# Delta-rule layer on one core: 64-token products in 64x64 tiles, convolution steps issued one block later

## The chip, the core and the metric

The kernel runs on one core of a Trainium2 chip. The core has a matrix engine (TensorE; PE in the profile), a vector engine (VectorE; DVE), an activation engine (ScalarE; ACT), a general engine (GpSimd; POOL) and SyncE (SP), which here does little but issue DMA transfers. Each engine works through its own instruction queue in order; they meet through semaphores. The metric is device microseconds for one execution, first to last instruction and a little around it. Before the change the median of three runs is 2928.5 us (2926.8 to 2933.6).

## What is computed

A model of two layers on 2 x 1024 tokens of width 256, all in float32: layer 0 adds a gated delta-rule attention and a mixture-of-experts layer to the residual, layer 1 a gated linear attention and a sparsified feed-forward. The change touches only the delta rule, which for each of 32 value heads (16 key heads, each shared by two value heads) is

```python
mixed = concat([q, k, v]); y = silu(causal_conv(mixed, conv_w, KSIZE=4))   # per channel
beta = sigmoid(b); g = -exp(A_log) * softplus(a + dt_bias)
q = l2norm(q) * DK ** -0.5; k = l2norm(k)                                  # repeated for 2 value heads
def step(S, inp):
    qt, kt, vt, gt, bt = inp
    S = S * exp(gt)[:, None, None]
    kv = einsum('hk,hkv->hv', kt, S)
    delta = (vt - kv) * bt[:, None]
    S = S + kt[:, :, None] * delta[:, None, :]
    return S, einsum('hk,hkv->hv', qt, S)
gated = core * silu(z); gated *= rsqrt(mean(gated ** 2) + EPS); out = (gated * norm_w) @ W_out
```

The kernel doesn't step through tokens. It takes 64 tokens at a time and solves what they do to one another with the inverse of a unit lower triangular 64x64 matrix.

## The kernel before

Layer 0's expert part runs from about 70 to 257 us of the span, the delta rule from 257 to about 2610, layer 1 after that.

The delta rule goes over 8 groups of heads (4 value heads, 2 key heads, written m). In a group the 1024 tokens of both batches are cut into 4 units of 256 tokens, a unit into 2 pairs, a pair into 2 chunks. A chunk holds 64 tokens of each batch: batch 0 on partitions 0 to 63 (`LO`), batch 1 on 64 to 127 (`HI`). That makes 64 pairs, 128 chunks. Every pair passes through these steps, in generators that give way after a few instructions:

- `conv_block`: four projections pj per pair (L152), copied by ScalarE into `raw` (L356) behind three old columns (GpSimd, L347), scaled by the last tap (ScalarE, L358), then three multiply-adds on VectorE (L363), then silu (L372, issued by the next block's `silu_pending`).
- `gates_part`: in odd pairs the sums of squares of q and k (`unit_sums`: products ssr, a copy, four transposes ss) and from them the norms on GpSimd (`unit_norms`, rn at L447); then two z projections.
- `pair_scores`: decay lb (scan L508, L510, L512), products kq, the matrices np (L526; index 0 keys by keys, index 1 queries by keys, which the output product uses), and DMAs on SyncE that lay np out anew: nat (L530), natd through DRAM (L536) and n8 (L540).
- `pair_lanes`: the inverse of all 8x8 diagonal blocks on VectorE (X at L558 to E at L582), spread by two DMAs (ed, U; L584, L586).
- `pair_inverse`: the ladder from 8 to 64: px, xs, pyt, U, and a transpose L of U at each rung (L603 to L645), the last rung with px (L660), xs (L663), pyt (L669) and copies into `invT`.
- `chunk_tokens`: keys by tokens, scaled (ktok, L688), values by tokens (vtok, L697).
- `chunk_state`: pks and pqs from state S (L716), four updates of vtok (L719), S times decay (GpSimd, L724), pf = invT x vtok (L734), f (ScalarE), pS (L743), po (L747), S plus pS (L754), qs, z (L758, L760).
- `chunk_output`, `chunk_project`: mean of squares (L765, ms at L775), root, scaling z (L782), transposes yT, projection out (L798), residual (L800).

pf multiplies with a 128x128 matrix whose two 64x64 blocks are the batches' inverses and whose other blocks are zero. po uses 64x64 blocks as they are, both batches at once.

`in_windows` (L823) sets the program's order. Each generator has a window in the pair's time (0 to 1), its steps are spread evenly over it, and the generator whose next step is due first issues it. The tile framework's scheduler then places each instruction on its engine; `tc.issue_after(x)` keeps what is issued inside it behind x on the engine. `k.anchor` is the latest convolution step; the scan (L508) and the first X (L558) are kept behind it. PSUM is one pool of 8 banks of 128x512, handed out in turn to every product (`ps_tile`).

Of the kernel before, what the change touches and what calls it, by code (L numbers as in the profile page):

```python
# [9 lines left out]
F32 = mybir.dt.float32  # L10
# [139 lines left out]
def project(k, ps, lhsT_of, rhs_of):  # L150
    for kt in range(KT):
        k.nc.tensor.matmul(ps, lhsT_of(kt), rhs_of(kt), start=(kt == 0), stop=(kt == KT - 1))  # L152
# [27 lines left out]
def delta_gates(k, pool, I):  # L180
# [66 lines left out]
    for b, rows in enumerate((LO, HI)):  # L247
        ps = ps_tile(k, f"sum_end{b}")
        nc.tensor.matmul(ps, k.ones[rows], flat(g)[rows], start=True, stop=True)
        nc.scalar.activation(flat(k.eEnd[:, b]), ps, AF.Exp)  # L250
        yield
# [75 lines left out]
def conv_block(k, pools, h, m, i):  # L327
# [31 lines left out]
    if h.part < NPART - 1:  # L359
        nc.gpsimd.tensor_copy(k.tails[:, at], raw[:, :, HALF // NB :])  # L360
    for j in range(KSIZE - 1):
        shifted = raw[:, :, j : j + HALF // NB]
        k.anchor = nc.vector.scalar_tensor_tensor(y, shifted, tap(j), y, ALU.mult, ALU.add).ins  # L363
        yield
    k.pending.append((out.rearrange("p (c b i) -> p b c i", b=NB, i=CT), chunks(y)))
# [10 lines left out]
def conv_part(k, pools, p, n):  # L376
# [9 lines left out]
    for v, m, i in blocks[n : n + 2]:  # L386
        if 0 <= v < NUNIT:
            yield from conv_block(k, pools, k.units[v], m, i)


def gates_part(k, pools, p):

    u, odd = divmod(p, 2)
    if odd and u + 1 < NUNIT:
# [3 lines left out]
        yield from unit_sums(k, pools, k.units[u + 1])  # L398
        unit_norms(k, pools, k.units[u + 1])
        yield  # L400
    if 0 <= p - 1 < NPAIR:
        for x in k.pairs[p - 1].chunks:
            chunk_gate(k, pools, x)
            yield


def chunk_gate(k, pools, x):
# [4 lines left out]
    project(k, ps, lambda kt: k.xnT[:, kt, t0 : t0 + P], lambda kt: w[:, kt].rearrange("p m c -> p (m c)"))  # L412
    x.z = pools.z.tile([P, HPG, P], F32, tag="z", name=f"z{x.name}")
    nc.scalar.activation(x.z.rearrange("p h d -> p (h d)"), ps, AF.Silu)

# [12 lines left out]
def unit_sums(k, pools, h):  # L428
# [7 lines left out]
    yield  # L436
    ps = ps_tile(k, f"ss{h.name}").rearrange("p (c a) -> p c a", c=UCHUNK)
    for c in range(UCHUNK):
        nc.tensor.transpose(ps[:, c, :], of_chunk(rows, c), k.ident)
# [49 lines left out]
def pair_scores(k, pools, pr):  # L489
# [8 lines left out]

    nc, wk, h = k.nc, pools.work, pr.h
# [110 lines left out]
def pair_inverse(k, pools, pr):  # L610
# [20 lines left out]
    nc.vector.transpose(flat(L), flat(U))  # L631
    yield
    for s in (3, 4):
# [11 lines left out]
        nc.vector.transpose(flat(L), flat(U))  # L645
# [7 lines left out]
    for n, r in enumerate(QUARTERS):  # L653
        (nc.gpsimd.tensor_copy, nc.scalar.copy)[n % 2](invT[r, :, r], U[r])
# [15 lines left out]
    for q, copy in ((0, nc.scalar.copy), (2, nc.vector.tensor_copy)):  # L670
        copy(invT[QUARTERS[q], :, QUARTERS[q + 1]], pyt[QUARTERS[q]])
# [3 lines left out]
def chunk_tokens(k, pools, x):  # L675

    nc, wk, h, c = k.nc, pools.work, x.h, x.c
    if not x.last:
# [22 lines left out]
def chunk_state(k, pools, x):  # L701

    nc, wk, h, c = k.nc, pools.work, x.h, x.c
# [5 lines left out]
    if not x.first:  # L709
        pks, pqs = four(k, f"pks{x.name}"), four(k, f"pqs{x.name}")  # L710
        for s, out in ((0, pks), (1, pqs)):
            for m in range(KPG):
                two = slice(2 * m, 2 * m + 2)
                for b, rows in halves:
                    q = of_chunk(h.kq[m][:, s], c, b)
                    nc.tensor.matmul(out[rows, two, :], q, k.S[:, b, two, :], start=True, stop=True)  # L716
        yield
        for i in range(HPG):
            nc.vector.scalar_tensor_tensor(  # L719
                x.v[:, i, :], pks[:, i, :], at(k.neG, i), x.v[:, i, :], ALU.mult, ALU.add  # L720
            )
# [10 lines left out]
    pf = four(k, f"pf{x.name}")  # L732
    for i in range(HPG):
        nc.tensor.matmul(pf[:, i, :], invT[:, i, :], x.v[:, i, :], start=True, stop=True)  # L734
    f = wk.tile([P, HPG, P], F32, tag="f", name=f"f{x.name}")
    nc.scalar.copy(f, pf)  # L736
    yield
    if not x.last:
        pS = [four(k, f"pS{x.name}_{b}") for b in range(NB)]
        for i in range(HPG):  # L740
            for b, rows in halves:
                for cols in (LO, HI):
                    nc.tensor.matmul(pS[b][cols, i, :], x.k[rows, i, cols], f[rows, i, :], start=True, stop=True)  # L743
# [721 lines left out]
```

## Time and profile before

| | us |
|---|---|
| median of three runs | 2928.5 (2926.8 to 2933.6) |
| profiled execution | 2937.13 |
| its span, first to last instruction | 2935.4 |
| mean granted TensorE clock | 0.969 |
| pj, 1024 matmuls | 529.5 busy |
| convolution steps L363, 768 | 692.6 busy, 188.0 idle ahead |
| pf, 1024 records | 153.0 busy, 29.8 idle ahead |
| po, 2048 records | 135.1 busy |
| pS, 3840 records | 132.5 busy, 12.6 idle ahead |
| px (L603), 8192 records | 102.1 busy, 143.1 idle ahead |
| ktok on GpSimd, 120 | 142.7 busy |
| np on VectorE, 128 | 82.0 busy |

"Busy" is the time in which the engine worked on that group. "Idle ahead" is the time that the engine stood still just before instructions of the group. TensorE splits an fp32 product into passes, which the profile lists as records of their own: one 128x128 by 128x128 product gives two. The records of one engine overlap a little (pipelining), so what a group takes of the path is read from its start to the start of the next group on the same engine. In a timeline a row reads: start us, duration us, engine, line, operation, output<-inputs, shape, count, and in brackets the idle time before it and who ended it.

### The profile page before, as it was taken

How to read it: one execution, taken by the hardware profiler on the slowest of the kernel's cores; microseconds unless marked ns; L12 is line 12 of the kernel's file. 1: busy time of each engine (PE TensorE's matmuls, PEld its weight loads, DVE VectorE, ACT ScalarE, POOL GpSimd, SP SyncE). 2: the span in 40 equal slices, each digit the busy share in tenths (PEclk: the TensorE clock that was granted, in tenths of full speed). 3: DMA queues.
4: the chain of work that ended last, by engine and by line, in shares of the span. 5: the costliest groups of instructions: out<-in, count | busy, mean ns of one | idle time of the engine just before them, and what ended most of it. 6: DMA issues, size and time to landing. Idle time of an engine off the chain costs nothing.

```text
span 2935.4 us, 87796 instructions
## 1 busy us (share of the span) xinstructions
PE 2642.3 (90%) x36502; PEld 1673.8 (57%) x36502; DVE 1938.2 (66%) x3845; ACT 1713.7 (58%) x4121; POOL 1542.9 (53%) x2690
## 2 busy tenths in 40 slices
PE   5998689999999899989998999999999989989997
PEld 2444356665666566656665666566555655654565
DVE  7652566766777677767776776677677767645544
ACT  4432566666666666666676666666666666544321
POOL 2222466666666666666666666566666666630000
PEclk9998899999999999999999999999999999999999
DMA  3001111111111111111111111111111111110000
GB/s 77 4 1 58 37 27 32 39 36 35 36 36 44 26 35 37 44 28 43 30 41 28 42 36 35 28 42 36 41 23 37 31 34 25 24 60 0 1 15 15
DMA packets 265966, 95.22 MB, mean 32 GB/s; under 512 B 220513, under 2 KB 244193, under 8 KB 265569
## 3 DMA queue, kind: packets, MB, share of 16 engines
q1 hardware_dynamic: 261872, 86.67, 13.2%
q8 instruction: 287, 4.70, 0.7%
q10 hardware_dynamic: 3696, 2.95, 0.4%
q14 instruction: 111, 0.90, 0.1%
HBM read 53.63 MB, written 27.53 MB: 28 GB/s over the span
## 4 chain that ended last, share of the span: by engine, by line
PE 49%; DVE 18%; POOL 13%; ACT 6%; issue 6%; DMA 4%; SPq 4%; DVEq 0%; POOLq 0%; ACTq 0%
PE pj L152 9%; DVE conv L363 5%; PE out L798 4%; PE z L152 4%; POOL rn L447 3%; PE pks L716 3%; POOL S L724 2%; PE pS L743 2%; SPq L540 2%; PE px L603 2%; PE pf L734 2%; DMA natd<-np 2%; PE y L1083 2%; PE pg L152 2%; DVE qs L758 2%
## 5 line engine op out<-in xcount | busy, mean ns | idle before, releaser
L363 DVE SCALAR_TENSOR_TENSOR conv<-raw,convw,conv 128x512 f32<-128x512 f32 x768 | 692.6, 903 | 188.0 <-ACT conv L358 127.7
L152 PE MATMUL pj<-xnT,w 128*128 128x512 f32 x1024 | 529.5, 643 | 8.7 <-DMA w<-in_W_qkvz 8.7
L152 PEld LDWEIGHTS pj<-xnT,w 128*128 128x128 f32 x1024 | 192.6, 201 | 193.2 <-issue 185.8
L719 DVE SCALAR_TENSOR_TENSOR vtok<-pks,neG,vtok 128x128 f32<-128x128 f32 x480 | 142.3, 343 | 218.4 <-PE pks L716 217.6
L724 POOL TENSOR_TENSOR S<-S,eEnd 128x512 f32<-128x512 f32 x224 | 261.5, 1184 | 31.9 <-PE pqs L716 20.8
L765 ACT ACTIVATE gsq<-z 128x128 f32<-128x128 f32 x512 | 156.8, 306 | 194.2 <-DVE z L760 186.2
L798 PE MATMUL out<-wo,yTs 128*128 128x256 f32 x1024 | 253.6, 391 | 1.4 <-ACT yTs L788 1.4
L152 PE MATMUL z<-wz,xnT 128*128 128x512 f32 x512 | 246.8, 605 | 0.0
L356 ACT COPY raw<-pj 128x512 f32<-128x512 f32 x256 | 148.0, 578 | 152.3 <-PE pj L152 139.3
L603 PE MATMUL px<-L,natm 32*32 32x32 f32 x8192 | 102.1, 200 | 143.1 <-DVE L L645 124.7
L347 POOL COPY raw<-tails 128x6 f32<-128x6 f32 x192 | 75.2, 392 | 249.1 <-DVE conv L363 242.6
L798 PEld LDWEIGHTS out<-wo,yTs 128*128 128x128 f32 x1024 | 187.6, 193 | 26.2 <-ACT yTs L788 1.9
L603 PEld LDWEIGHTS px<-L,natm 32*32 32x32 f32 x8192 | 88.5, 111 | 168.5 <-issue 83.1
L734 PE MATMUL pf<-vtok,invT 128*128 128x128 f32 x1024 | 153.0, 287 | 29.8 <-DVE vtok L719 27.3
L358 ACT ACTIVATE conv<-pj,convw 128x512 f32<-128x512 f32 x256 | 177.0, 692 | 0.0
L754 DVE TENSOR_TENSOR S<-S,pS 128x512 f32<-128x512 f32 x224 | 145.8, 682 | 33.4 <-POOL S L724 25.5
L729 ACT ACTIVATE qs<-pqs,neG 128x128 f32<-128x128 f32 x480 | 136.5, 367 | 48.9 <-PE pqs L716 48.9
L734 PEld LDWEIGHTS pf<-vtok,invT 128*128 128x128 f32 x1024 | 129.9, 192 | 45.7 <-DVE vtok L719 30.8
L447 POOL TENSOR_TENSOR rms<-ms,mhalf 128x4 f32<-128x4 f32 x128 | 148.7, 1162 | 9.9
L782 POOL TENSOR_TENSOR z<-z,rms 128x512 f32<-128x512 f32 x128 | 142.8, 1116 | 10.0
L743 PE MATMUL pS<-f,ktok 64*64 64x128 f32 x3840 | 132.5, 275 | 12.6 <-ACT f L736 12.6
L688 POOL TENSOR_TENSOR ktok<-kt,wend 128x512 f32<-128x512 f32 x120 | 142.7, 1189 | 0.8 <-ACT kt L684 0.8
(323 smaller groups left out, 5775.9 us busy)
## 6 DMA issues: line engine op xcount, KB each, us to landing
lb<-grows SPq DMA_DIRECT2D x128, 128.0 KB
natd<-np SPq DMA_DIRECT2D x128, 128.0 KB
w<-in_W_qkvz SPq DMA_DIRECT2D x16, 512.0 KB
nat<-np SPq DMA_DIRECT2D x256, 32.0 KB
n<-natd SPq DMA_DIRECT2D x512, 4.0 KB
ed<-E SPq DMA_DIRECT2D x64, 128.0 KB
U<-ed SPq DMA_DIRECT2D x64, 128.0 KB
wz<-in_W_qkvz SPq DMA_DIRECT2D x16, 256.0 KB
```

Source lines behind the costliest of these rows:

```text
L152: k.nc.tensor.matmul(ps, lhsT_of(kt), rhs_of(kt), start=(kt == 0), stop=(kt == KT - 1))
L356: nc.scalar.copy(chunks(raw[:, :, KSIZE - 1 :]), pv)
L358: nc.scalar.activation(chunks(y), pv, AF.Copy, scale=tap(KSIZE - 1))
L363: k.anchor = nc.vector.scalar_tensor_tensor(y, shifted, tap(j), y, ALU.mult, ALU.add).ins
L447: nc.gpsimd.tensor_tensor(out, x, k.mhalf[:, 0 : x.shape[1]], ALU.pow)
L603: k.nc.tensor.matmul(out[r, i, :], lhsT[r, i, :], rhs[r, i, :], start=True, stop=True)
L724: nc.gpsimd.tensor_tensor(k.S[:, b], k.S[:, b], bcast(k.eEnd[:, b, t, h.h0 : h.h0 + HPG], 2, P), ALU.mult)
L734: nc.tensor.matmul(pf[:, i, :], invT[:, i, :], x.v[:, i, :], start=True, stop=True)
L743: nc.tensor.matmul(pS[b][cols, i, :], x.k[rows, i, cols], f[rows, i, :], start=True, stop=True)
L754: nc.vector.tensor_tensor(k.S[:, b], k.S[:, b], pS[b], ALU.add)
L765: nc.scalar.activation(sq, x.z[:, i, :], AF.Square, accum_out=x.sumsq[:, i : i + 1])
L798: nc.tensor.matmul(po[:, 0:D], x.yT[:, i, :], wo[:, i, :], start=(i == 0), stop=(i == HPG - 1))
```

## The change

1. pf and po become eight products each in 64x64 tiles, at all four places of the array: rows by the half r that the inputs lie in, columns by the half r^m that the output goes to. Both are written to one PSUM tile `fo` of two banks (bank m holds key head m) from a pool of its own; the other pool shrinks from 8 to 6 banks, and each stage has its own. invT keeps only its 64x64 blocks.
2. As key head 1's results land in the other half, its state is kept with the halves crossed: `eEnd` is written in four operations, pks and pqs read `S[:, b ^ m]`. Half of ktok and half of the second np are computed into helper tiles (ktoko, npo), by two operations of half the size, and two DMAs of SyncE each carry them to the other half: 120 chunks and 64 pairs.
3. The convolution steps of a block are issued after the next block's evacuation (`convolve`), and behind `k.chain`: the ladder's last L or the last vtok update. conv1 is cut into conv1 and conv2.
4. In odd pairs a z projection is issued between ssr and the transposes ss, which stay behind it on TensorE.

Instructions in the program, before and after: TensorE matmuls 19075, 19587; VectorE tensor_tensor 1656, 1720; GpSimd tensor_tensor 1753, 1873; SyncE DMA issues 1235, 1603; ScalarE activations two more.

The diff at its core; hunks of the same kind and small ones are left out:

```diff
@@ -247,7 +248,10 @@
     for b, rows in enumerate((LO, HI)):
         ps = ps_tile(k, f"sum_end{b}")
         nc.tensor.matmul(ps, k.ones[rows], flat(g)[rows], start=True, stop=True)
-        nc.scalar.activation(flat(k.eEnd[:, b]), ps, AF.Exp)
+        by_key = lambda a: a.rearrange("p (t g m j) -> p t g m j", t=NTILE, g=NGROUP, m=KPG)
+        for m in range(KPG):
+            mine = by_key(flat(k.eEnd[:, b ^ m]))[:, :, :, m]
+            nc.scalar.activation(mine, by_key(ps)[:, :, :, m], AF.Exp)
         yield
     for name in ("neG", "nrev"):
         nc.vector.tensor_scalar(sums[name], sums[name], -1.0, None, ALU.mult)
@@ -358,11 +362,24 @@
     nc.scalar.activation(chunks(y), pv, AF.Copy, scale=tap(KSIZE - 1))
     if h.part < NPART - 1:
         nc.gpsimd.tensor_copy(k.tails[:, at], raw[:, :, HALF // NB :])
+    yield from convolve(k)
+    k.projected = y, raw, tap, (out.rearrange("p (c b i) -> p b c i", b=NB, i=CT), chunks(y))
+def convolve(k):
+    if not k.projected:
+        return
+    y, raw, tap, silu = k.projected
     for j in range(KSIZE - 1):
         shifted = raw[:, :, j : j + HALF // NB]
-        k.anchor = nc.vector.scalar_tensor_tensor(y, shifted, tap(j), y, ALU.mult, ALU.add).ins
+        with ExitStack() as behind:
+            if k.chain:
+                behind.enter_context(k.tc.issue_after(k.chain))
+            k.anchor = k.nc.vector.scalar_tensor_tensor(y, shifted, tap(j), y, ALU.mult, ALU.add).ins
         yield
-    k.pending.append((out.rearrange("p (c b i) -> p b c i", b=NB, i=CT), chunks(y)))
+    k.projected = None
+    k.pending.append(silu)
 def silu_pending(k):
@@ -383,25 +400,34 @@
         blocks = [(u + 1, 1, 0), (u + 1, 1, 1), (u + 1, 0, 2), (u + 1, 0, 3)]
     else:
         blocks = [(u + 1, 0, 0), (u + 1, 0, 1), (u, 1, 2), (u, 1, 3)]
-    for v, m, i in blocks[n : n + 2]:
+    for v, m, i in blocks[n : n + count]:
         if 0 <= v < NUNIT:
             yield from conv_block(k, pools, k.units[v], m, i)
+        elif k.projected:
+            yield from convolve(k)
+            silu_pending(k)
 def gates_part(k, pools, p):
     u, odd = divmod(p, 2)
+    chunks = k.pairs[p - 1].chunks if 0 <= p - 1 < NPAIR else []
+    gate = None
     if odd and u + 1 < NUNIT:
         for m in range(KPG):
             unit_squares(k, pools, k.units[u + 1], m)
             yield
-        yield from unit_sums(k, pools, k.units[u + 1])
+        rows = unit_sums(k, pools, k.units[u + 1])
+        yield
+        for x in chunks[0:1]:
+            gate = chunk_gate(k, pools, x)
+            yield
+        unit_turned(k, k.units[u + 1], rows, gate)
         unit_norms(k, pools, k.units[u + 1])
         yield
-    if 0 <= p - 1 < NPAIR:
-        for x in k.pairs[p - 1].chunks:
-            chunk_gate(k, pools, x)
-            yield
+    for x in chunks[1:] if gate else chunks:
+        chunk_gate(k, pools, x)
+        yield
 def chunk_gate(k, pools, x):
@@ -433,10 +460,18 @@
         nc.tensor.matmul(ps[r, :], k.ones[:, r], sq, start=True, stop=True)
     rows = pools.sq.tile([P, HALF], F32, tag="sq", name=f"ssr{h.name}")
     nc.scalar.copy(rows, ps)
-    yield
+    return rows
+def unit_turned(k, h, rows, ahead):
     ps = ps_tile(k, f"ss{h.name}").rearrange("p (c a) -> p c a", c=UCHUNK)
-    for c in range(UCHUNK):
-        nc.tensor.transpose(ps[:, c, :], of_chunk(rows, c), k.ident)
+    with ExitStack() as behind:
+        if ahead:
+            behind.enter_context(k.tc.issue_after(ahead))
+        for c in range(UCHUNK):
+            k.nc.tensor.transpose(ps[:, c, :], of_chunk(rows, c), k.ident)
     h.ss = ps.rearrange("p c (m i r) -> p c m i r", m=KPG, i=2)[:, :, :, :, 0]
@@ -521,11 +557,15 @@
     yield
     pr.np = pools.np.tile([P, 2, PC, HPG, CT], F32, tag="np", name=f"np{pr.name}")
     pairs = lambda a: a.rearrange("p x (m j) i -> p (x m) j i", m=KPG)
-    for s in range(2):
-        by = kq[:, :, :, s].rearrange("p x m i -> p (x m) i")
-        nc.vector.tensor_tensor(pairs(pr.np[:, s]), pairs(lb), bcast(by, 2, 2), ALU.mult)
-        if s == 0:
-            yield
+    by = kq[:, :, :, 0].rearrange("p x m i -> p (x m) i")
+    nc.vector.tensor_tensor(pairs(pr.np[:, 0]), pairs(lb), bcast(by, 2, 2), ALU.mult)
+    yield
+    other = wk.tile([P, PC, 2, CT], F32, tag="npo", name=f"npo{pr.name}", bufs=1)
+    for m, out in enumerate((pr.np[:, 1, :, 0:2], other)):
+        two = slice(2 * m, 2 * m + 2)
+        nc.vector.tensor_tensor(out, lb[:, :, two], bcast(kq[:, :, m, 1], 2, 2), ALU.mult)
+    for rows, across in ((LO, HI), (HI, LO)):
+        nc.sync.dma_start(pr.np[across, 1, :, 2:4], other[rows])
     for n, r in enumerate(QUARTERS):
         nc.sync.dma_start(pr.nat[r], pr.np[r, 0, :, :, QUARTERS[n % 2]])
@@ -628,7 +668,7 @@
     U = pr.U
     join = masked(3)
     L = new("L", 3)
-    nc.vector.transpose(flat(L), flat(U))
+    k.chain = nc.vector.transpose(flat(L), flat(U)).ins
     yield
     for s in (3, 4):
         px = part(k, f"px{s}_{pr.name}", B)
@@ -651,7 +691,7 @@
     invT = pr.invT.rearrange("p x h c -> p (x h) c")
     full = pr.np[:, 0].rearrange("p x h c -> p (x h) c")
     for n, r in enumerate(QUARTERS):
-        (nc.gpsimd.tensor_copy, nc.scalar.copy)[n % 2](invT[r, :, r], U[r])
+        (nc.gpsimd.tensor_copy, nc.scalar.copy)[n % 2](invT[r, :, QUARTERS[n % 2]], U[r])
     yield
     px = part(k, f"px5_{pr.name}", B)
     for i in range(PH):
@@ -683,9 +724,12 @@
         kt = wk.tile([P, KPG, P], F32, tag="kt", name=f"kt{x.name}", bufs=1)
         nc.scalar.copy(kt, pk[:, 0:KPG, :])
         x.k = wk.tile([P, HPG, P], F32, tag="ktok", name=f"ktok{x.name}")
-        pair = lambda a: a.rearrange("p (m i) c -> p m i c", m=KPG)
-        wend = h.wend[:, c, :].rearrange("p (m i) -> p m i", m=KPG)
-        nc.gpsimd.tensor_tensor(pair(x.k), bcast(kt, 2, 2), bcast(wend, 3, P), ALU.mult)
+        other = wk.tile([P, 2, P], F32, tag="ktoko", name=f"ktoko{x.name}")
+        for m, out in ((1, other), (0, x.k[:, 0:2])):
+            wend = h.wend[:, c, 2 * m : 2 * m + 2]
+            nc.gpsimd.tensor_tensor(out, bcast(kt[:, m], 1, 2), bcast(wend, 2, P), ALU.mult)
+        for rows, across in ((LO, HI), (HI, LO)):
+            nc.sync.dma_start(x.k[across, 2:4], other[rows])
         yield
     pv = four(k, f"pv{x.name}")
     for i in range(HPG):
@@ -713,12 +761,12 @@
                 two = slice(2 * m, 2 * m + 2)
                 for b, rows in halves:
                     q = of_chunk(h.kq[m][:, s], c, b)
-                    nc.tensor.matmul(out[rows, two, :], q, k.S[:, b, two, :], start=True, stop=True)
+                    nc.tensor.matmul(out[rows, two, :], q, k.S[:, b ^ m, two, :], start=True, stop=True)
         yield
         for i in range(HPG):
-            nc.vector.scalar_tensor_tensor(
+            k.chain = nc.vector.scalar_tensor_tensor(
                 x.v[:, i, :], pks[:, i, :], at(k.neG, i), x.v[:, i, :], ALU.mult, ALU.add
-            )
+            ).ins
         if not x.last:
             for b in range(NB):
                 nc.gpsimd.tensor_tensor(
@@ -729,22 +777,33 @@
             nc.scalar.activation(qs[:, i, :], pqs[:, i, :], AF.Copy, scale=at(k.neG, i))
         yield
-    pf = four(k, f"pf{x.name}")
-    for i in range(HPG):
-        nc.tensor.matmul(pf[:, i, :], invT[:, i, :], x.v[:, i, :], start=True, stop=True)
+    fo = k.psum2.tile([P, KPG, 2, 2, P], F32, tag="fo", name=f"fo{x.name}")
+    pf, po = fo[:, :, 0], fo[:, :, 1]
+    across = lambda r, m: halves[r ^ m][1]
+    for i in range(2):
+        for m in range(KPG):
+            for r, rows in halves:
+                n = 2 * m + i
+                nc.tensor.matmul(pf[across(r, m), m, i, :], invT[rows, n, :], x.v[rows, n, :], start=True, stop=True)
     f = wk.tile([P, HPG, P], F32, tag="f", name=f"f{x.name}")
-    nc.scalar.copy(f, pf)
+    by_key = lambda a: a.rearrange("p (m i) d -> p m (i d)", m=KPG)
+    flat = lambda a: a.rearrange("p m i d -> p m (i d)")
+    nc.scalar.copy(by_key(f), flat(pf))
     yield
     if not x.last:
-        pS = [four(k, f"pS{x.name}_{b}") for b in range(NB)]
+        pS = [four(k, f"pS{x.name}_{r}") for r in range(NB)]
         for i in range(HPG):
-            for b, rows in halves:
+            for r, rows in halves:
                 for cols in (LO, HI):
-                    nc.tensor.matmul(pS[b][cols, i, :], x.k[rows, i, cols], f[rows, i, :], start=True, stop=True)
-    po = four(k, f"po{x.name}")
-    for i in range(HPG):
-        for b, rows in halves:
-            nc.tensor.matmul(po[rows, i, :], x.pair.np[rows, 1, x.at, i, :], f[rows, i, :], start=True, stop=True)
+                    nc.tensor.matmul(pS[r][cols, i, :], x.k[rows, i, cols], f[rows, i, :], start=True, stop=True)
+    for i in range(2):
+        for m in range(KPG):
+            for r, rows in halves:
+                n = 2 * m + i
+                nc.tensor.matmul(
+                    po[across(r, m), m, i, :], x.pair.np[rows, 1, x.at, n, :], f[rows, n, :], start=True, stop=True
+                )
     yield
     if not x.last:
         for b in range(NB):
@@ -753,11 +812,11 @@
             else:
                 nc.vector.tensor_tensor(k.S[:, b], k.S[:, b], pS[b], ALU.add)
     yield
-    no = po
+    no = flat(po)
     if not x.first:
-        nc.vector.tensor_tensor(qs, qs, po, ALU.add)
-        no = qs
-    nc.vector.tensor_tensor(x.z, no, x.z, ALU.mult)
+        nc.vector.tensor_tensor(by_key(qs), by_key(qs), no, ALU.add)
+        no = by_key(qs)
+    nc.vector.tensor_tensor(by_key(x.z), no, by_key(x.z), ALU.mult)
     yield
     x.sumsq = pools.small.tile([P, HPG], F32, tag="sumsq", name=f"sumsq{x.name}")
     for i in range(HPG):
@@ -895,14 +955,13 @@
             work = []
             add = lambda kind, lo, hi, steps, *before: work.append((kind, lo, hi, steps, before))
             prefetch(k, pools, p)
-            if p == NPAIR - 1:
-                silu_pending(k)
             if p == -2:
                 for q in (0, 1):
                     pair_decays(k, pools, pair(q))
-            add("conv0", 0.0, 0.475, conv_part(k, pools, p, 0))
-            add("conv1", 0.475, 0.95, conv_part(k, pools, p, 2), "conv0")
-            add(f"gates{p % 2}", 0.65, 1.0, gates_part(k, pools, p), "output1", "conv0")
+            add("conv0", 0.0, 0.475, conv_part(k, pools, p, 0, 2))
+            add("conv1", 0.475, 0.71, conv_part(k, pools, p, 2, 1), "conv0")
+            add("conv2", 0.71, 0.95, conv_part(k, pools, p, 3, 1), "conv1")
+            add(f"gates{p % 2}", 0.65, 1.0, gates_part(k, pools, p), "output1", "conv1")
             if pair(p):
                 add("scores", 0.0, 0.45, pair_scores(k, pools, pair(p)))
                 add("lanes", 0.65, 0.9, pair_lanes(k, pools, pair(p)), "scores")
@@ -1360,7 +1419,7 @@
     k = Ctx()
     k.nc, k.tc = nc, tc
     k.keep = ctx.enter_context(tc.tile_pool(name="keep", bufs=1))
-    k.psum = ctx.enter_context(tc.tile_pool(name="psum", bufs=8, space=bass.MemoryType.PSUM))
+    psum = lambda name, bufs: tc.tile_pool(name=name, bufs=bufs, space=bass.MemoryType.PSUM)
     k.res = k.keep.tile([P, NTILE, D], F32, tag="res", name="res")
     k.mv = k.keep.tile([P, NTILE, 2], F32, tag="mv1", name="mv1")
@@ -1388,10 +1449,13 @@
         k.gates = scope.enter_context(tc.tile_pool(name="d_gates", bufs=1))
         k.dram = scope.enter_context(tc.tile_pool(name="d_dram", bufs=1, space=bass.MemoryType.DRAM))
         expert_layer(k, I)
-        delta_layer(k, I)
+        early.close()
+        with psum("psum1", 6) as k.psum, psum("psum2", 1) as k.psum2:
+            delta_layer(k, I)
     with ExitStack() as scope:
         pool = lambda name, bufs: scope.enter_context(tc.tile_pool(name=name, bufs=bufs))
+        k.psum = scope.enter_context(psum("psum3", 8))
         pools = Pools()
         pools.const, pools.work, pools.h = pool("l1_const", 1), pool("l1_work", 2), pool("l1_h", 2)
         xn = pools.const.tile([P, NTILE, D], F32, tag="xn1", name="xn1")
```

More of the change, by code (lines that the diff above doesn't have):

```diff
@@ L151, in project @@
     for kt in range(KT):
-        k.nc.tensor.matmul(ps, lhsT_of(kt), rhs_of(kt), start=(kt == 0), stop=(kt == KT - 1))
+        last = k.nc.tensor.matmul(ps, lhsT_of(kt), rhs_of(kt), start=(kt == 0), stop=(kt == KT - 1)).ins
+    return last
 def thin_projection(k, pool, name, w, m):
@@ L373, in silu_pending, with conv_part @@
     k.pending = []
-def conv_part(k, pools, p, n):
+def conv_part(k, pools, p, n, count):
     u, odd = divmod(p, 2)
@@ L411, in chunk_gate @@
     t0 = (h.t0 + x.c) * P
-    project(k, ps, lambda kt: k.xnT[:, kt, t0 : t0 + P], lambda kt: w[:, kt].rearrange("p m c -> p (m c)"))
+    last = project(k, ps, lambda kt: k.xnT[:, kt, t0 : t0 + P], lambda kt: w[:, kt].rearrange("p m c -> p (m c)"))
     x.z = pools.z.tile([P, HPG, P], F32, tag="z", name=f"z{x.name}")
     nc.scalar.activation(x.z.rearrange("p h d -> p (h d)"), ps, AF.Silu)
+    return last
 def unit_squares(k, pools, h, m):
@@ L644, in pair_inverse @@
         L = new("L", s + 1)
-        nc.vector.transpose(flat(L), flat(U))
+        k.chain = nc.vector.transpose(flat(L), flat(U)).ins
         if s < 4:
@@ L670, in pair_inverse @@
     for q, copy in ((0, nc.scalar.copy), (2, nc.vector.tensor_copy)):
-        copy(invT[QUARTERS[q], :, QUARTERS[q + 1]], pyt[QUARTERS[q]])
+        copy(invT[QUARTERS[q], :, QUARTERS[1]], pyt[QUARTERS[q]])
     yield
@@ L855, in delta_layer @@
         k.tails = const.tile([P, 4 * KPG, NB, KSIZE - 1], F32, tag="tails", name="tails")
-        k.invT = [const.tile([P, PC, HPG, P], F32, tag=f"invT{i}", name=f"invT{i}") for i in range(2)]
+        k.invT = [const.tile([P, PC, HPG, CT], F32, tag=f"invT{i}", name=f"invT{i}") for i in range(2)]
         k.S = const.tile([P, NB, HPG, P], F32, tag="S", name="S")
@@ L874, in delta_layer @@
         k.I, k.weights, k.steps, k.pending = I, {}, {}, []
+        k.projected = k.chain = None
         k.units = [unit_of(u) for u in range(NUNIT)]
@@ L1373, in two_layers @@
     k.xnT = k.keep.tile([P, KT, N], F32, tag="xnT", name="xnT")
+    early = ctx.enter_context(ExitStack())
+    k.psum = early.enter_context(psum("psum0", 8))
     with tc.tile_pool(name="ln0", bufs=2) as pool:
```

## The prediction

> **What bounds the kernel now.** I read the page first: the busy shares, then the chain that ended last.
>
> ```profile
> PE 2642.3 (90%) x36502; PEld 1673.8 (57%) x36502; DVE 1938.2 (66%) x3845; ACT 1713.7 (58%) x4121; POOL 1542.9 (53%) x2690
> ...
> PE 49%; DVE 18%; POOL 13%; ACT 6%; issue 6%; DMA 4%; SPq 4%; DVEq 0%; POOLq 0%; ACTq 0%
> ```
>
> TensorE is 90% busy, yet only half of the chain is TensorE; a fifth is VectorE and an eighth GpSimd. So TensorE is nearly the bound, with other engines taking turns in every pair. The waits say where:
>
> ```profile
> PE px L603 <- DVE L L645: 124.7, 64, 3.9
> ...
> DVE X L558 <- DMA n<-natd: 30.3, 26, 2.4
> ...
> PE pf L734 <- DVE vtok L719: 27.3, 28, 1.3
> ```
>
> The columns are total us, times, longest. TensorE waits once per pair (64) for the ladder's last transpose L; 28 times for vtok; VectorE waits 26 times for the n8 loads. The last row matters most below, for it stands at the end of SyncE's queue. Now one pair, from its first np on VectorE at 1588.60: TensorE, then SyncE.
>
> ```profile
> 1584.15 1.10 PE L743 MATMUL pS<-f,ktok 64*64 64x128 f32 x32
> 1585.08 1.05 PE L747 MATMUL po<-f,np 64*64 64x128 f32 x16
> ...
> 1592.24 0.75 PE L603 MATMUL px<-L,natm 32*32 32x32 f32 x64 [1.91 <-DVE L L645]
> ```
>
> ```profile
> 1589.31 2.66 SPq L530 DMA_DIRECT2D nat<-np  x4
> 1592.02 1.25 SPq L536 DMA_DIRECT2D natd<-np  x2
> 1593.36 1.19 SPq L596 DMA_DIRECT2D lb<-grows  x2
> 1596.36 3.63 SPq L540 DMA_DIRECT2D n<-natd  x8
> ```
>
> The pS row gives the price of four tiles abreast: 32 records in 0.93 us (start to next start), where po, two abreast, has 16 in 0.98. The SyncE rows are a chain: nat 0.7 us after np, natd at 3.4, n8 at 7.8, its last issue done at 11.4; VectorE begins X at 1603.19, 14.6 after np, having idled 2.08. Behind X VectorE's order is fixed, and it ends in what TensorE needs for pyt5 (L669):
>
> ```profile
> 1605.31 0.42 DVE L582 TENSOR_TENSOR E<-X,place 128x256 f32<-128x256 f32 x1
> 1605.65 1.53 DVE L363 SCALAR_TENSOR_TENSOR conv<-raw,convw,conv 128x512 f32<-128x512 f32 x2
> 1607.10 1.28 DVE L754 TENSOR_TENSOR S<-S,pS 128x512 f32<-128x512 f32 x2
> 1608.30 0.68 DVE L758 TENSOR_TENSOR qs<-qs,po 128x512 f32<-128x512 f32 x1
> 1609.01 0.43 DVE L663 COPY xs<-px 32x256 f32<-32x256 f32 x1
> ```
>
> In odd pairs GpSimd has the unit's norms (rn), the decay and an output scale in front of S:
>
> ```profile
> 1573.22 2.90 POOL L447 TENSOR_TENSOR rn<-sse,mhalf 128x16 f32<-128x16 f32 x1
> ...
> 1584.60 2.04 POOL L724 TENSOR_TENSOR S<-S,eEnd 128x512 f32<-128x512 f32 x2
> ```
>
> From sse (1571.98) to the end of S (1586.64) this takes 14.7 us, and state, qs, z and the next np wait for it.
>
> **Period of a pair.** Over 62 pairs from np to np: 36.03 us, of which 22.26 from np to pyt5 and 13.77 from pyt5 to the next np. By position in the group of eight the first part is 21.4, 19.9, 23.5, 28.2, 21.1, 21.5, 21.0, 21.3 us; positions 3, 5 and 7 have second parts of 16.2 to 17.1, the others 10.0 to 13.0.
>
> **The change, part by part.**
>
> *Tiles.* pf takes 0.89 us per chunk (8 records, start to next start), po 0.98. In four tiles each is 16 records: half of the pS row, 0.46. Saving 0.43 + 0.52 = 0.95 per chunk, 128 chunks: 122 us of TensorE time. That is the most that it can give. The other bound is that the tiles don't overlap better than po's do now: then pf costs 0.98 (a loss of 0.09) and po 0.98 (nothing), a loss of 12 us. I take 0.46, as pS is the same tile form.
>
> [...]
>
> *PSUM.* fo takes two banks of eight, one buffer; the other pool keeps six. In the compiled order of both kernels the reuse distance goes from 8 to 6 or 7 tiles; the tile before it has been read by then, so I cost it at nothing; if not, a wait the size of an eviction (0.59, the f copy) in a chunk would be 76 us.
>
> *Crossed np.* Second np operation: one 128x512 (0.68) becomes two 128x256 (0.41 each, from U at L643): +0.14 on VectorE. Two DMAs more per pair on SyncE, of 64 partitions, behind the first nat and before the other three nat, natd and n8. An issue costs 0.63 (natd: 1.25 for two). They wait for the second half product, which ends some 0.25 after nat's first issue. So natd, n8, X move back by 2 x 0.63 + 0.25 = 1.5 us in every pair. Lower bound nil (a pair where VectorE is late at X anyhow), upper bound 3 us (landing and queueing as for natd->n8, whose wait is 3.1).
>
> *Convolution.* The three steps are issued a block later. They no longer wait for ACT (127.7 us of VectorE idle), and are put behind L and vtok, so the px wait falls from 1.2 to 2.0 to about 0.6 (pyt to px through U 0.41 and L 0.43 less the yT that lies between), and the 1.25 before pf goes, in some 22 of the odd pairs. In the compiled order the two steps between E and S (1.53) leave that place. Raw head copies on GpSimd stop waiting for the steps: they hold GpSimd's queue by 6 us ahead of rn once or twice in a group.
>
> *First part after.* np to X: undisturbed pairs have 13.3 to 14.2; plus 1.5, 15.3. X to the end of xs: 6.25 above, less 1.45 for the steps, 4.8; pyt5 starts 0.15 to 0.3 later: 20.4. TensorE's own path would be 20.7 (typical) less pf and po (0.95) and the px wait (1.2): 18.6. So VectorE's chain sets the end, at 20.4, and TensorE waits 1.8 before pyt5. Over the eight positions: 177.9 before, 163.2 after, 14.7 less. Of position 3's 7.8 among them I count only 3.0: in the compiled order GpSimd's output scale, ms to z, there stands ahead of rn, and it takes 4.8 us (1579.78 to 1584.60 in the pair above). That leaves 10 us per group.
>
> *Second part.* Odd: sse comes 1.7 us later (ss now stands behind a z projection, 1.72), rn starts without the raw wait, GpSimd's chain stays 13.5; no gain. Even: pf and po give 0.95, but np stands behind S, qs and z on VectorE; zero taken, 0.95 x 4 as the upper bound. The ssr-to-ss wait (0.71 x 31 = 22 us) falls in odd pairs, hence hidden too.
>
> *Crossed ktok.* GpSimd: one of 1.04 becomes two of 0.73 (natm's form): +0.42, behind S in its order; hidden, since pS comes later; uncovered it costs 120 x 0.42 = 50 us. Two SyncE issues per chunk (1.25) lie in SyncE's free stretch from 1608 to 1622; the wait for ktok stands ahead of the next nat, with about 0.7 us to spare in odd pairs. eEnd's two more operations run once: nothing.
>
> *Sum.* 8 groups x 10 = 80 us. The profiled execution is 2937 (span 2935.4), 0.3% above the median of 2928.5; after: 2857 profiled, 2849 on the median's scale.
>
> **The rivals.**
>
> *TensorE stays the bound and takes all of it.* 122 (tiles) + 22 (ss) + 25 (pf's wait) = 169: 2760. For it: 90% busy, windows of 350 us at 92%. Against: even now pyt5 starts 0.14 after xs in many pairs, so that path is shared. Chance 0.22.
>
> *SyncE's queue becomes the bound (the slower side).* The crossed DMAs of np and the wait for GpSimd's ktok stand in order before natd and n8, and X to xs to pyt5 follows. Each microsecond beyond the 1.5 is worth 64 us in 64 pairs; 80/64 = 1.25 more, 2.75 in all, eats the gain. With ktok's wait and both its issues in front of nat (1.75 more): 2849 + 112 = 2961. For it: X waits for n8 already; the margin is 0.7. Against: SyncE is idle for half of a pair. Chance 0.13.
>
> *Tiles do not pack.* No saving on TensorE, but the waits still go: TensorE's path is then 20.7 + 0.1 - 1.2 = 19.6, still under 20.4, so only even second parts and places where TensorE is ahead lose: of the 80 about a third, 2880. Against: the pS row. Chance 0.10.
>
> *Nothing comes out:* the freed time is given back at pyt5 and S; 2928. Chance 0.05. My forecast has 0.50.
>
> **How the numbers follow.** A change under 0.2% can't be told from none here. Faster: 0.50 + 0.22 + 0.10 = 0.82; same 0.05; slower 0.13. Low end: all of position 3's stall (4.8) and the even second parts (3.8) gone as well, 8 x 8.6 = 69 more, 2780, and some of the first rival, 2770. High end: 2.5 us in place of 1.5 before X, 64 more, 2913; 2915. Left out: the rival at 2961, half of the first, the 2928.
>
> **What would show it.** fo's groups at 0.46 to 0.56 per 16 records, not 0.9; the px wait at some 40 us in place of 125; TensorE waiting for xs (L663) before pyt5 in most pairs, a new row of 60 to 120 us; X's wait for n8 well over 30; natd 4.9 after np; TensorE busy near 2525. The forecast is wrong if X stays at 13 to 14 after np (then nearer 2780), or if SyncE's nat starts over 1 us after np.

## The result, and the profile after

The changed kernel takes 2962.9 us (median of four runs, 2958.5 to 2967.6) against 2927.7 before: a ratio of 1.0115, with a 95% interval of 1.0095 to 1.0135. It is slower; the forecast was 2849, and its range ended at 2915.

The first lines of the page after, busy shares and the chain that ended last:

```profile
PE 2626.4 (89%) x37526; PEld 1578.4 (53%) x37526; DVE 1986.0 (67%) x3909; ACT 1721.2 (58%) x4123; POOL 1619.3 (55%) x2810
...
PE 38%; DVE 22%; POOL 13%; SPq 9%; issue 6%; DMA 6%; ACT 6%; DVEq 0%; ACTq 0%; POOLq 0%
```

TensorE is busy 15.9 us less and the span is 30.5 us longer, so it stands still 46.4 us more. Its share of the chain fell from 49% to 38%; SyncE's queue went from 4% to 9%, VectorE from 18% to 22%. The busy time would have fallen further, but part of it ran slower: between the first and the last np the clock rows of the trace show 119.5 us at half clock before (25 stretches) and 232.1 after (49). TensorE was busy in 96.8 and 201.9 us of them. From start to next start a pj record takes 0.854 us in the half-clock stretches after and 0.429 outside them (medians of 91 and 648). At that rate half of the time is lost, so the added 105 us cost an estimated 53, and the work, at full clock, is about 15.9 + 53 = 69 us less. The waits after (us, times, longest):

```profile
PE px L643 <- DVE L L685: 113.1, 64, 4.6
...
DVE L L671 <- DMA U<-ed: 91.6, 62, 4.3
...
PE ss L474 <- ACT ssr L462: 49.1, 30, 2.0
...
PE pyt L709 <- DVE xs L703: 43.5, 38, 3.7
...
DVE X L598 <- DMA n<-natd: 32.1, 13, 5.6
```

The px wait stayed (124.7 before). The wait of pyt for xs is new, and the ss wait doubled (22.6 before) instead of going. VectorE's wait for U at the ladder's first L (L671) is nearly new too: 8.5 us before. The wait of pf for vtok did go, from 27.3 to 1.9. What stands ahead of px is seen on VectorE, in front of the px of the rows further below:

```profile
1556.61 1.29 DVE L813 TENSOR_TENSOR S<-S,pS 128x512 f32<-128x512 f32 x2 [1.59 <-PE pS L799]
...
1559.58 0.45 DVE L685 STREAM_TRANSPOSE L<-U 128x256 f32<-128x256 f32 x1
```

Between the two rows stand qs, z and U; no convolution step does. On TensorE's timeline the tiles do what they were meant to:

```profile
1525.70 0.67 PE L788 MATMUL fo<-vtok,invT 64*64 64x128 f32 x16
1526.30 1.99 PE L857 MATMUL out<-wo,yTs 128*128 128x256 f32 x8
...
1560.18 0.93 PE L643 MATMUL px<-L,natm 32*32 32x32 f32 x64 [1.84 <-DVE L L685]
1561.04 3.39 PE L152 MATMUL pj<-xnT,w 128*128 128x512 f32 x4
```

From start to next start the former pf now takes 0.598 us in the median and po 0.547. The last row shows the price of standing still: after a wait of 1.84 us the pj projection takes 3.39 instead of 1.98, and the clock rows have half clock from 1560.49 to 1563.90. All 49 half-clock stretches but one follow a 3.4 us stretch in which TensorE was busy for at most 0.58 of the time (the one: 0.63; before: at most 0.51). SyncE's queue in a pair whose np began at 1516.26:

```profile
1519.79 1.11 SPq L732 DMA_DIRECT2D ktok<-ktoko  x2
1520.99 0.65 SPq L570 DMA_DIRECT2D nat<-np  x1
1521.74 1.28 SPq L568 DMA_DIRECT2D np<-npo  x2
1523.07 2.90 SPq L570 DMA_DIRECT2D nat<-np  x3
1526.02 1.25 SPq L576 DMA_DIRECT2D natd<-np  x2
1527.36 1.19 SPq L636 DMA_DIRECT2D lb<-grows  x2
1529.10 3.63 SPq L580 DMA_DIRECT2D n<-natd  x8
```

nat could have gone at 1516.9; ktok's two DMAs stand ahead of it and wait for GpSimd until 1519.79. natd begins 9.8 us after np (3.4 before), and X 19.2 us after.

By pair (means over 62, from the first np; "end of pyt5" is the end of the last ladder product, which the new wait splits; positions in the group are counted from 0, so positions 0, 2, 4 and 6 are the even pairs):

| | natd | X | end of E | end of xs | end of pyt5 | period | even, odd |
|---|---|---|---|---|---|---|---|
| before | 3.56 | 14.41 | 17.60 | 21.35 | 22.98 | 36.03 | 33.57, 38.49 |
| after | 5.76 | 16.06 | 20.04 | 21.73 | 22.83 | 36.55 | 35.35, 37.75 |
| convolution order alone (e4) | 3.52 | 14.30 | 19.46 | 21.35 | 22.50 | 35.83 | 34.22, 37.43 |
| tiles without crossings (e5) | 3.55 | 14.51 | 19.44 | 21.33 | 22.52 | 35.95 | 34.08, 37.82 |

### The profile page after: what moved, and what is told of

The parts are those of the page before. It is cut to its first block, busy times and chain, and to the rows that moved or that the text cites. A ratio compares the mean times of both kernels' runs of the same rounds, so it can differ in the third digit from the quotient of the medians.

```text
span 2965.9 us, 90669 instructions
## 1 busy us (share of the span) xinstructions
PE 2626.4 (89%) x37526; PEld 1578.4 (53%) x37526; DVE 1986.0 (67%) x3909; ACT 1721.2 (58%) x4123; POOL 1619.3 (55%) x2810
## 4 chain that ended last, share of the span: by engine, by line
PE 38%; DVE 22%; POOL 13%; SPq 9%; issue 6%; DMA 6%; ACT 6%; DVEq 0%; ACTq 0%; POOLq 0%
PE pj L152 8%; DVE conv L379 4%; SPq L580 4%; DVE S L813 3%; SPq L570 3%; PE out L857 3%; DMA natd<-np 3%; POOL rn L482 3%; PE pks L764 2%; POOL S L772 2%; PE y L1142 2%; DMA n<-natd 2%; PE px L643 2%; PE pg L152 2%; PE base L152 2%
## 5 line engine op out<-in xcount | busy, mean ns | idle before, releaser
L379 DVE SCALAR_TENSOR_TENSOR conv<-raw,convw,conv 128x512 f32<-128x512 f32 x768 | 683.8, 921 | 20.9 <-DMA wz<-in_W_qkvz 13.3
L152 PE MATMUL pj<-xnT,w 128*128 128x512 f32 x1024 | 558.9, 674 | 8.6 <-DMA w<-in_W_qkvz 8.6
L772 POOL TENSOR_TENSOR S<-S,eEnd 128x512 f32<-128x512 f32 x224 | 272.9, 1238 | 87.4 <-PE pqs L764 55.2
L152 PE MATMUL z<-wz,xnT 128*128 128x512 f32 x512 | 260.9, 634 | 5.7 <-ACT conv L362 5.5
L364 POOL COPY tails<-raw 128x6 f32<-128x6 f32 x192 | 60.0, 313 | 217.6 <-ACT raw L360 188.8
L389 ACT ACTIVATE v<-conv 128x512 f32<-128x512 f32 x128 | 81.4, 636 | 158.2 <-DVE conv L379 158.0
L482 POOL TENSOR_TENSOR rn<-sse,mhalf 128x16 f32<-128x16 f32 x32 | 93.0, 2906 | 116.6 <-DVE sse L495 116.6
L152 PEld LDWEIGHTS z<-wz,xnT 128*128 128x128 f32 x512 | 92.2, 195 | 102.6 <-issue 73.0
L764 PE MATMUL pks<-S,kq 128*64 128x256 f32 x960 | 142.1, 418 | 3.4 <-DVE S L813 3.4
L834 POOL TENSOR_TENSOR ms<-sumsq,q 128x4 f32<-128x4 f32 x128 | 61.1, 477 | 152.7 <-ACT gsq L824 152.6
```

The source lines that it names most:

```text
L152: last = k.nc.tensor.matmul(ps, lhsT_of(kt), rhs_of(kt), start=(kt == 0), stop=(kt == KT - 1)).ins
L379: k.anchor = k.nc.vector.scalar_tensor_tensor(y, shifted, tap(j), y, ALU.mult, ALU.add).ins
L482: nc.gpsimd.tensor_tensor(out, x, k.mhalf[:, 0 : x.shape[1]], ALU.pow)
L764: nc.tensor.matmul(out[rows, two, :], q, k.S[:, b ^ m, two, :], start=True, stop=True)
L772: nc.gpsimd.tensor_tensor(k.S[:, b], k.S[:, b], bcast(k.eEnd[:, b, t, h.h0 : h.h0 + HPG], 2, P), ALU.mult)
```

## The experiments

Each was timed against the kernel before on the same chip; the medians of before lay between 2924.6 and 2926.6. The diffs are against the kernel named.

**One part at a time.** e1, against after:

```diff
-    for rows, across in ((LO, HI), (HI, LO)):
-        nc.sync.dma_start(pr.np[across, 1, :, 2:4], other[rows])
...
+    for rows, across in ((LO, HI), (HI, LO)):
+        nc.sync.dma_start(pr.np[across, 1, :, 2:4], other[rows])
```

> The changed kernel with the two crossing DMAs of np issued behind the eight n8 loads on SyncE instead of behind the first nat. Theory S (SyncE's queue: the crossing DMAs push natd, n8 and X back, which then sets pyt5): natd about 3.8 us after np instead of 5.5, X about 14.5 instead of 16.0, and with 1.5 us less in the 32 even pairs at least, 2963 - 48 = 2915; half-clock windows in the delta rule near 35 instead of 49. Theory V (VectorE's order: the later convolution steps, which X and the scan stand behind, make X late; no idle time is shown before X in most pairs): natd is earlier, X is not, 2955 to 2965.

Measured: 2948.9 (ratio 1.0081, 1.0063 to 1.0098), 14 us below after. natd 4.0 after np, X 14.8. X did come earlier, by 1.3 us, so the crossing was in its way; but the end of xs only by 0.2 (21.54). Theory S was right about X and wrong about its worth (2915 was expected).

e2 gives after the convolution of before; e3 gives it ss directly behind ssr as well.

> The changed kernel with the convolution as before (steps right after their own block's evacuation, not kept behind L or vtok, two windows); tiles, crossings and the z projection between ssr and ss stay. Theory S: the crossings are still ahead of natd, so X stays at 15.5 to 16 after np and the time near 2960, perhaps worse, since px waits longer again (2975). Theory V: X returns to 14 to 15 and the tiles' saving comes out: 2880 to 2900.

> The kernel before with the tiles and crossings alone (convolution and ss as before). Theory S: 2960 to 2980, slower than before, with natd 5.5 us after np. Theory V: 2870 to 2890, faster than before by about half of the 94 us that fo's rows save on TensorE.

Measured: e2 3029.8 (1.0334 to 1.0372), e3 2982.2 (1.0175 to 1.0211). Tiles and crossings alone cost 56 us, as theory S had it; theory V falls. e2 was worse than either expected.

e4 and e8 start from before: the later steps with, and without, z ahead of ss.

> The kernel before with the later convolution steps and the z projection between ssr and ss alone (no tiles, no crossings). Theory S: nothing stands ahead of natd, px's wait falls, so faster than before: 2890 to 2910. Theory V: slower than before, 2940 to 2960, X later than 14.4 after np though natd stays at 3.4.

> The kernel before with the later convolution steps alone, ss directly behind ssr as before. If the z projection between them gains what its wait showed (22 us in 31 places), this is slower than with it (2921) by 10 to 20. If the norms on GpSimd set the odd pairs, putting z ahead of ss delays them by 1.7 us, and this is faster by up to 30 x 1.7 = 50: 2870 to 2915.

Measured: e4 2920.8 (0.9974 to 1.0000), e8 2978.3 (1.0169 to 1.0213). The order of the convolution, with z ahead of ss, is worth 5 us and not the 20 to 40 that theory S asked for. Without z between, TensorE stands 105 us ahead of ss in e8 against 47 in e4, as much as the difference of 57; with the convolution as before, the same edit loses 48 (e2 against e3). Why it turns there was not tried.

Why the order gave so little is seen on VectorE in e4, in front of pyt5:

```profile
1297.02 1.19 DVE L376 SCALAR_TENSOR_TENSOR conv<-raw,convw,conv 128x512 f32<-128x512 f32 x1
1298.48 0.66 DVE L590 COPY X<-n 128x4 f32<-128x4 f32 x1 [0.26 <-DMA n<-natd]
...
1299.12 1.42 DVE L540 TENSOR_TENSOR_SCAN lb<-lb,floor 128x512 f32<-128x512 f32 x1
...
1302.97 0.43 DVE L614 TENSOR_TENSOR E<-X,place 128x256 f32<-128x256 f32 x1
1303.32 1.28 DVE L786 TENSOR_TENSOR S<-S,pS 128x512 f32<-128x512 f32 x2
1304.51 0.68 DVE L790 TENSOR_TENSOR qs<-qs,po 128x512 f32<-128x512 f32 x1
1305.22 0.43 DVE L695 COPY xs<-px 32x256 f32<-32x256 f32 x1
```

The steps are gone from behind E, but the scan, which is kept behind the latest step, came forward with them. Before, it stands behind xs in 61 of 62 pairs; in e4 it stands between X and the end of E in 60. So X to the end of E takes 5.16 us instead of 3.19 (means), and xs ends at 21.35 after np, as before. The step ahead of X in these rows delays nothing: VectorE still waits 0.26 us for n8 after it.

The scan left a gap behind xs. The ladder's first L, before and after:

```profile
1610.74 1.22 DVE L508 TENSOR_TENSOR_SCAN lb<-lb,floor 128x512 f32<-128x512 f32 x1
1611.88 0.42 DVE L631 STREAM_TRANSPOSE L<-U 128x256 f32<-128x256 f32 x1
```

```profile
1541.64 0.69 DVE L819 TENSOR_TENSOR z<-qs,z 128x512 f32<-128x512 f32 x1
1543.42 0.45 DVE L671 STREAM_TRANSPOSE L<-U 128x256 f32<-128x256 f32 x1 [1.08 <-DMA U<-ed]
```

VectorE now stands still until the DMA of U has landed: 88.1 us in e4, 91.6 after, 25.1 in e3, 8.5 before. The later steps wait behind it, for `k.chain` is set at every L, the first too. In even pairs the stretch from the end of pyt5 to the next np grew from 11.08 to 11.94 us in e4 and not in e3 (10.96). That the wait for U makes this growth is argued: no run takes the wait away.

**The crossings.** e5 is after with ktok and np computed whole and nothing carried; e6 keeps ktok's crossing, e7 np's.

```diff
-    for rows, across in ((LO, HI), (HI, LO)):
-        nc.sync.dma_start(pr.np[across, 1, :, 2:4], other[rows])
...
-        for rows, across in ((LO, HI), (HI, LO)):
-            nc.sync.dma_start(x.k[across, 2:4], other[rows])
```

> The changed kernel with nothing carried to the other half: ktok and the second np are computed whole as before, and the 368 crossing DMAs are gone; the output product and the state update of key head 1 then use rows of the wrong batch. Tiles, convolution order and z before ss stay. Theory S (the crossings eat what the tiles give): the saving of about 0.73 us per chunk comes out against the kernel with the convolution order alone (2921), 2830 to 2860. Theory L (TensorE's work is not on the path once the waits are gone: X, xs, S on VectorE and GpSimd set the period): 2905 to 2925, with TensorE idle some 80 us longer than in that kernel.

> As the run without any crossing, but ktok is still split and carried by two DMAs per chunk; only the crossing of np is gone (the output product of key head 1 uses rows of the wrong batch). Theory S with the np DMAs as the main part: 2850 to 2880. Theory L: 2915 to 2935. If ktok's wait on SyncE matters, natd stays over 4 us after np at some positions of the group and the time is 10 to 20 above the run without crossings.

> As the run without any crossing, but np is still split and carried by two DMAs per pair behind the first nat; only ktok's crossing is gone (the state of key head 1 uses rows of the wrong batch). Theory S: X still 1.5 us late in every pair, 2930 to 2950. Theory L: the same, since X is on the path in both; the distance to the run without crossings is the price of np's crossing, 15 to 40.

Measured: e5 2931.8 (1.0005 to 1.0033), e6 2936.2 (1.0023 to 1.0052), e7 2940.8 (1.0039 to 1.0071). With nothing crossed the tiles still gain nothing; against e4 (2920.8) they lose 11. So the crossings explain 31 us (2963 less 2932): ktok's alone about 4, np's alone about 9, the rest only with both in SyncE's queue. The pages of e4 and e5, first group:

```profile
PE 2659.1 (91%) x36502; PEld 1675.3 (57%) x36502; DVE 2000.6 (69%) x3845; ACT 1716.2 (59%) x4121; POOL 1604.8 (55%) x2690
```

```profile
PE 2607.9 (89%) x37526; PEld 1569.5 (54%) x37526; DVE 1984.0 (68%) x3845; ACT 1718.3 (59%) x4123; POOL 1604.5 (55%) x2690
```

The spans are 2918.7 and 2920.2 (e5's profiled execution was its fastest, so the loss of 11 is not in these two pages). TensorE is busy 51 us less and idle 53 us more. Its half-clock time rose from 140 to 205 us; it was busy in 121 and 179 of these, which costs an estimated 29. So of the tiles' 80 us 53 came back as standing still and 29 as slow clock. Most of the standing still is ahead of px, first in e4, then in e5:

```profile
PE px L635 <- DVE L L677: 73.3, 64, 4.1
```

```profile
PE px L639 <- DVE L L681: 111.5, 64, 4.8
```

The order alone had brought this wait down from 124.7. With the tiles TensorE reaches px earlier and waits 38 us more for the same L.

**What holds the period.** e9 and e10 leave one convolution step of three out (`if j != 1` around it), with tiles (e5) and without (e4).

> The run without crossings (tiles kept, 2932) with one of the three convolution steps of every block left out: the convolution lacks one tap, and VectorE has 256 operations of 0.7 us less, 4 per pair. Theory L (VectorE's order sets the period, so TensorE's saving could not show): with 3 us per pair taken off VectorE the time falls, and it falls further than in the kernel without tiles, since TensorE is then nearer to the bound: 2780 to 2830, at least 40 below the run with the same step left out and no tiles. If the period is set by GpSimd and by the length of the chain from state to state, both light runs fall alike and the tiles are still worth nothing.

> The kernel before with the later convolution steps and z before ss (2921), no tiles, with one of the three convolution steps of every block left out: the convolution lacks one tap. Theory L: TensorE becomes the bound, 2850 to 2880. If TensorE bound it already, no change, 2915 to 2921.

Measured: 2882.9 (0.9828 to 0.9858) and 2898.1 (0.9882 to 0.9911). With VectorE eased the tiles are worth 15 us, less than the 40 expected: VectorE is one part of what hides them. It is not eased alone, however. The page of e9:

```profile
PE 2586.1 (90%) x37526; PEld 1570.3 (54%) x37526; DVE 1734.1 (60%) x3589; ACT 1711.1 (59%) x4123; POOL 1485.0 (51%) x2690
```

GpSimd has the same 2690 instructions as in e5 and is busy 1485.0 us instead of 1604.5. Its decay of S, for one, takes 1.10 us each instead of 1.22. In e10 it is 1488.8 instead of 1604.8.

e11 and e12 add work to TensorE, to after and to e5:

```diff
+        if s == 4:
+            nc.tensor.matmul(ps, k.ident, k.xnT[:, 0, 0:512], start=True, stop=True)
         blocks32(k, px, join, L)
```

> The changed kernel with one more product (128x128 by 128x512 of constants, 0.9 us, its result overwritten) ahead of each px that waits for the ladder's second transpose, 64 in all: TensorE works in half of that wait instead of standing still. Theory C (standing still drops TensorE's clock, and the half-clock stretches are a cost of their own): half-clock windows in the delta rule fall from 49 to 30 to 38 and the time falls by 15 to 40, to 2925 to 2950, though 60 us of work were added. Otherwise: no change where the wait is longer, and up to 20 slower where it is shorter, 2963 to 2985.

> The run without crossings (2932) with the same 64 products ahead of px. Theory C: half-clock windows from 45 to about 30, 2895 to 2920, below the kernel without tiles (2921), as far as the clock and not the order ate the tiles' saving. Otherwise 2932 to 2950.

Measured: 2950.7 (1.0053 to 1.0090), 12 us faster than after with 64 products more (TensorE busy 2665.8 us instead of 2626.4); and 2928.9 (0.9998 to 1.0023), no different from e5 (busy 2656.9 instead of 2607.9). Half-clock time fell from 232 to 184 us in the first and from 205 to 184 in the second. TensorE has time to spare in both; that the clock alone made the 12 us was not isolated, and in e12 it made nothing.

e13 to e16 put GpSimd's output scale (ms to z) of a unit's last chunk behind the state's decay S (`k.decayed` is its latest multiply), in e4, e5, e1 and before:

```diff
+    with ExitStack() as behind:
+        if k.decayed and x.c == UCHUNK - 1:
+            behind.enter_context(k.tc.issue_after(k.decayed))
...
```

> The kernel with the later convolution steps and z before ss (2921, no tiles), with one order more: the output scale of a unit's last chunk (ms to z, 4.8 us on GpSimd) stands behind the state's decay S instead of ahead of it, in the pairs that also have the norms. Theory G (GpSimd's chain from sse to S sets those 32 pairs, of 37.4 us in every kernel so far): S, qs, z and np come up to 4.8 us earlier in 24 to 32 pairs until TensorE or VectorE binds, 2800 to 2870. Otherwise 2910 to 2930.

> The tiles without crossings (2932), with the same order of the output scale behind S. Theory G: with GpSimd out of the way TensorE is nearer to the bound in half of the pairs, so the tiles now show: 20 to 50 below the same order without tiles. If VectorE's chain takes over at once, the two are equal within 10.

> The changed kernel with np's crossing behind n8 (2949) and the same order. Theory G: falls as much as the others, to 2830 to 2890, below the kernel before; what remains above the run without crossings is the price of ktok's crossing and of the later pS, 10 to 20.

> The kernel before with this order alone. Theory G: 2820 to 2880; the odd pairs fall from 38.5 to 35 or 36 us, the even ones stay at 33.6.

Measured: e13 2899.2 (0.9878 to 0.9917), e14 2878.5 (0.9810 to 0.9846), e15 2899.7 (0.9888 to 0.9922), e16 2923.5 (0.9979 to 0.9998). GpSimd in e13:

```profile
1272.78 1.04 POOL L544 TENSOR_TENSOR lb<-lb,nb 128x512 f32<-128x512 f32 x1
1273.78 2.04 POOL L756 TENSOR_TENSOR S<-S,eEnd 128x512 f32<-128x512 f32 x2
1275.77 0.20 POOL L810 TENSOR_TENSOR ms<-sumsq,q 128x4 f32<-128x4 f32 x1
...
1280.26 1.04 POOL L817 TENSOR_TENSOR z<-z,rms 128x512 f32<-128x512 f32 x1
```

S now follows the decay lb directly. The odd pairs fall from 37.4 to 36.5 us in e13 and from 37.8 to 36.3 in e14. The tiles are worth 21 us there, where they had cost 11; the sign turned with one order on GpSimd. Theory G has the direction right in e13, e14 and e15, with 22, 53 and 49 us, but e13, e15 and e16 all miss the ranges that it named. In before itself the order gives 3 us, the odd pairs staying at 38.4; why was not tried.

e17 adds the fill to e15; e18 eases VectorE and GpSimd together.

> The changed kernel with np's crossing behind n8, the output scale behind S (2900), and the 64 extra products ahead of px that the earlier fill run had. If the clock is a cost of its own, as it was there (12 us), 2880 to 2895; px's wait is shorter now (about 49 us in place of 113 without the first), so the products may stand on the path instead: 2900 to 2925.

> The tiles without crossings and the output scale behind S (2878), with one of the three convolution steps of every block left out (the convolution lacks one tap, key head 1's rows are of the wrong batch). Theory: VectorE and GpSimd together hold the period, so with both eased it falls well below either alone (2883 and 2878): 2800 to 2840. If something else binds there already, no more than 15 below 2878.

Measured: e17 2892.8 (0.9863 to 0.9905), e18 2800.5 (0.9539 to 0.9584). The page of e18:

```profile
PE 2561.4 (91%) x37526; PEld 1559.1 (56%) x37526; DVE 1749.3 (62%) x3589; ACT 1713.5 (61%) x4123; POOL 1500.8 (54%) x2690
```

Leaving out the step gave 49 us against e5, the order on GpSimd 53, both 131: more than their sum. So each hides part of the other, and together they hold the period; TensorE is back at 91%. The same kernel without tiles was not run with both, so what the tiles are worth there is not known.

The versions that do the whole computation and beat both kernels by about 1% are e13, e15 and e17, at 2893 to 2900; their intervals overlap.

## Why the prediction was wrong

The sum had one term: 10 us less per group, 1.25 per pair, in the part from np to pyt5, and nothing in the rest of the pair. Measured to the end of pyt5, the first part fell by 0.15 us (70 us of the miss over 64 pairs), and the second grew by 0.67 (43 us).

- **X to the end of xs, the step that failed first**: "X to the end of xs: 6.25 above, less 1.45 for the steps, 4.8". Measured 5.67, and in e4, which has the order alone, 7.05. The base was one pair; the mean before is 6.94. And the forecast took the two steps off and put nothing in their place, while the scan, kept behind the latest step, moved up: into the ladder in e4, and after the change ahead of X in 45 of 62 pairs and into the ladder in 17. The end of xs came at 21.73 instead of 21.35, and not at 20.1.
- **np to X**: 15.3 forecast, 16.1 measured; natd 4.9 forecast, 5.8 measured. Where no ktok stands ahead natd starts at 5.4, also in e7, which carries np alone: 1.8 later than before, not 1.5. The two crossing issues took 1.3 us as counted, and the three nat behind them 0.4 more than before. At position 2 of the group ktok's wait came on top: nat starts at 3.4 and natd at 8.2. That was the slower rival's mechanism, and nat over 1 us after np was a sign named for the forecast being wrong, but e5 to e7 give all crossings together 31 us, of 114 between forecast and result. That the rival's figure of 2961 lies so near is luck.
- **The px wait**: 40 us forecast, 113 measured. L stands behind S, qs and z on VectorE, not behind the convolution alone: with the order by itself (e4) the wait is still 73. The tiles bring it back up, since TensorE comes to it earlier (e5, 111.5).
- **Second part**: zero forecast, 0.67 us per pair more measured, nearly all in even pairs (11.08 to 12.25; odd 15.03 to 15.18). Of the 1.17 in even pairs e4 has 0.86: they come with the later steps, and VectorE waits for U there, though that this wait is the cause is argued only.
- **A cost left out**: half-clock time. The forecast let TensorE wait 1.8 us ahead of pyt5 at no price; the half-clock stretches doubled from 25 to 49. That is an estimated 53 us of TensorE time, though not all on the path (e12).
- **Tiles**: right in kind, mis-sized by a quarter. Saving per chunk 0.95 forecast, 0.73 measured (0.60 and 0.55 instead of 0.46 each), 94 us of TensorE time. Sixteen records take 0.60 and 0.55 us where po's sixteen took 0.98, with two row halves writing each bank in both kernels, so the rival that the tiles do not pack falls. What keeps them 0.09 to 0.14 us above the 0.46 no run isolates.
- **PSUM**: nothing forecast, and little found. TensorE has one new wait on an eviction, z behind ScalarE's conv, 5.5 us in 11 places (9.2 in e5). No run has the tiles with eight banks.
- Right was that TensorE would not set the end; the rival in which it takes the whole saving is out by 200 us. e5, e9, e14 and e18 show what hides it: VectorE's order and GpSimd's chain, together. Why the tiles alone lose 11 us (e5 against e4) was not isolated.

## What to carry to other kernels

An engine at 90% can still be a follower (here TensorE, with 49% of the chain): before work is taken from it, count how often the chain passes through that work, and try the gain by adding work to it. A step moved out of one gap in an engine's order must be found again in the next one (here the scan, with X to the end of E at 5.16 us instead of 3.19); read the new order as a whole. Transfers that wait for another engine belong behind those that do not, when they share a queue (np's crossing behind n8 gave 14 us in e1).

## What the runs showed of the hardware

This is read from the two traces, before and after, and from the experiments. TensorE's clock rows, 66 before and 122 after, all begin a multiple of 3.41 us after the first of their trace. The counts that follow are of such 3.41 us stretches at full clock, between the first and the last np. In the changed kernel one in which TensorE was busy for less than 0.45 of the time was followed by half clock in 30 cases of 30, one with 0.45 to 0.65 in 19 of 46, and one with more in none of 526. Before, it was 14 of 15, 11 of 36 and none of 575. After the change the longest idle time within the stretch ahead was under 2 us in 27 of the 49 cases (0.87 in one, 1.23 to 1.99 in the others). After one of 1.84 us pj took 3.39 us instead of 1.98. 64 more products made one kernel 12 us faster (e11) and left another as it was (e12). With a third of the convolution steps taken off VectorE, GpSimd was busy 119.5 us less on the same 2690 instructions (1485.0 in e9, 1604.5 in e5). Of the changed kernel's DMAs of 64 partitions, np's two took 1.28 us of SyncE per pair and ktok's two 1.14 per chunk (medians of 64 and 120); natd's two had taken 1.25 in the trace before.
